# Layer norm's rows: two VectorE instructions, or GpSimd's offset and ScalarE, chosen by the planner

## The chip, the cores and the metric

The kernel runs on one core of a Trainium2 chip. The metric is the device time of one execution in microseconds (us), the median over runs.

## The reference

One decoder layer in fp32 with pre-norm residuals: 32 sequences of 256 tokens, width 256. Cut to what matters:

```python
def _layernorm(x, axis=-1, eps=1e-05):
    m = jnp.mean(x, axis=axis, keepdims=True)
    v = jnp.var(x, axis=axis, keepdims=True)
    return (x - m) / jnp.sqrt(v + eps)

x = x + _L0_attn_ref(_layernorm(x), Wq, Wk, Wv, Ws, Wg, Wo, qconv_w, kconv_w, vconv_w, gnorm_w)
x = x + _L0_xattn_ref(_layernorm(x), ctx_1024, ctx_1024, mask, W_q, W_k, W_v, W_proj, b_proj)
x = x + _L0_ffn_ref(_layernorm(x), gate_w, Wu, Wv, Wo)
```

The first step is a gated causal linear attention with short convolutions of q, k and v (4 heads), the second a cross attention of 16 heads over 77 context rows, the third a mixture of 8 experts of which each token takes the best 2. Each begins with a layer norm without weights, so there are 3 x 32 = 96 norms of 256 rows by 256 columns.

## The kernel before

The tokens of one sequence lie as two tiles of 128 partitions by 256 columns (NTT = 2). Three kinds of stage run over the sequences: `self_attention` (5 sequences in flight), `cross_attention` (3 in flight) and `experts` (two sequences at a time, the last two alone). Each stage is written as a Python generator. Before every piece of work it yields what it wants to use, as an engine and a cost in ns, or a list of such wishes between which it may be put.

A planner (`Flow`) runs these generators against a small model of the engines: at each step it starts the wish that could begin first. Where a thread offers a list, it takes the wish that would end first by the model, in which `LATER` adds 700 ns to VectorE's and 500 ns to ScalarE's end. `BOTH` means VectorE and `PAIR` GpSimd, each holding a port that the two share. `best_order` lays the whole kernel out 70 times with shifted ranks of the stages, keeps the order that ends first by the model, and `decoder_layer` then writes the instructions out in that order. So the order on every engine follows from the planner's costs, and a changed cost or choice anywhere can move instructions everywhere.

The layer norm is `layernorm_T`. Per tile, VectorE makes the statistics (`ln_st`, `ln_mv`, lines 690 and 691). `rsqrt` lets GpSimd add eps and take the power -0.5 (`rs_r`, lines 670 and 671). GpSimd then makes the offset `ln_off` = -mean x rstd (line 696, two small instructions), and ScalarE makes the row `ln_h` = x x rstd + offset (line 702, one pass per tile). `turn_to` transposes `ln_h` on TensorE into `hT_ps` (line 680), and `copy` moves that to SBUF as `hT_a`, `hT_x` or `hT_e`, on ScalarE (line 638) or VectorE (line 640), as the planner finds. The projections, the queries or the experts' products read it from there.

Other names that matter here: `y` (the convolution's taps, line 824 on VectorE, or `tap` on ScalarE with a sum on GpSimd), `RzT` (running sums at line 912 and their reciprocals at line 918), `E` (a clamp, line 900, on VectorE or GpSimd), `cap` (a mask, line 1119), `cv_qk` and `cv_v` (line 840), the softmax `s` of the cross attention (ScalarE, line 1211; its product with `s_rs` at line 647 on VectorE or GpSimd), and the routing of the experts (`wt_ps`, line 1362). Line 647 holds all the products which `combine` places on VectorE or GpSimd.

Of the kernel before, what the change touches and what calls it, by code (L numbers as in the profile page):

```python
# [12 lines left out]
F32 = mybir.dt.float32  # L13
U8 = mybir.dt.uint8
AF = mybir.ActivationFunctionType
ALU = mybir.AluOpType
# [3 lines left out]
P = 128  # L20
# [23 lines left out]
PE, DVE, ACT, POOL, SP = "PE", "DVE", "ACT", "POOL", "SP"  # L44

BOTH, PAIR = "BOTH", "PAIR"
# [28 lines left out]
def act(columns, pointer=False):  # L75
    return 75 + 0.82 * columns + (80 if pointer else 0)
# [286 lines left out]
def decoder_layer(  # L363
# [27 lines left out]
    nc = tc.nc  # L391
    B, T, D = x.shape
    S2 = ctxT.shape[2]
    ND = D // P
    NTT = T // P
# [4 lines left out]
    small = ctx.enter_context(tc.tile_pool(name="small", bufs=6))  # L400
# [23 lines left out]
    def lay_out(flow, nc, const, work, small, dram, psum):  # L424


        def take(tag, uses=1, name=None):
            shape = shapes[tag]

            kind = tag if isinstance(shape, tuple) else "f"  # L430
            buf = yield Take(kind, uses)
            dtype = F32
            if kind == tag:
                dtype = shape[2] if len(shape) > 2 else F32
                shape = shape[1]
            buf.tile = work.tile(
                shape, dtype, tag=f"{kind}{buf.slot}", name=name or tag, bufs=1
            )
            return buf
# [194 lines left out]
        def copy(to, source, columns, scale=None):  # L634

            engine, _ = yield [(ACT, act(columns)), (DVE, dve(columns))]
            if engine == ACT:
                nc.scalar.activation(to, source, AF.Copy, scale=1.0 if scale is None else scale)  # L638
            elif scale is None:
                nc.vector.tensor_copy(to, source)  # L640
            else:
                nc.vector.tensor_scalar(to, source, scale, None, ALU.mult)
# [23 lines left out]
        def rsqrt(var, n):  # L666

            r = small.tile([P, n], F32, tag=f"rs_r{n}", name="rs_r")
            yield POOL, 700 + 155 * n
            nc.gpsimd.tensor_scalar(r, var, EPS, None, ALU.add)  # L670
            nc.gpsimd.tensor_tensor(r, r, mhalf[:, :n], ALU.pow)  # L671
            return r

        def turn_to(src, tag, done):

            ps = yield from fill("brief", turns(4), tag)
            pv = halves(ps.tile)
            for c in range(ND):
                for t in range(2):
                    nc.tensor.transpose(pv[:, c, ts(t, P)], src[:, t, ts(c, P)], ident)  # L680
            done.drop()
            return ps, pv

        def layernorm_T(xt, hT):

            st = small.tile([P, NTT, 6], F32, tag="ln_st", name="ln_st")
            mv = small.tile([P, NTT, 2], F32, tag="ln_mv", name="ln_mv")
            for t in range(NTT):
                yield DVE, 550
                nc.vector.bn_stats(st[:, t, :], xt[:, t, :])  # L690
                nc.vector.bn_aggr(mv[:, t, :], st[:, t, :])  # L691
            rstd = yield from rsqrt(mv[:, :, 1], NTT)
            off = small.tile([P, NTT], F32, tag="ln_off", name="ln_off")
            yield POOL, 460
            for t in range(NTT):
                nc.gpsimd.tensor_scalar(  # L696
                    off[:, t : t + 1], mv[:, t, :1], rstd[:, t : t + 1], -1.0, ALU.mult, ALU.mult
                )
            h = yield from take("h", name="ln_h")
            for t in range(NTT):  # L700
                yield ACT, act(D) + 205
                nc.scalar.activation(  # L702
                    h.tile[:, t, :], xt[:, t, :], AF.Identity, bias=off[:, t : t + 1],
                    scale=rstd[:, t : t + 1],
                )
            ps, pv = yield from turn_to(h.tile, "hT_ps", h)
            yield from copy(hT, pv, 512)
            ps.drop()
# [79 lines left out]
        def self_attention(n):  # L788
# [3 lines left out]
            xt = xs[n].tile  # L792
            hT = yield from take("hT_a", 4)
            yield from layernorm_T(xt, hT.tile)
            ready = [flow.event() for _ in range(2)]
            prods = [None, None]
# [308 lines left out]
        def cross_attention(n):  # L1105
# [47 lines left out]
            xt = xs[n].tile  # L1153
            hT = yield from take("hT_x")
            yield from layernorm_T(xt, hT.tile)
            ps = None
            for c in range(ND):
# [122 lines left out]
        def experts(n, count):  # L1280
# [6 lines left out]
            for b in range(count):  # L1287
                yield crossed[n + b]
                yield from layernorm_T(xs[n + b].tile, hT.tile[:, :, b * T : (b + 1) * T])
# [297 lines left out]
```

## Time and profile before

| what | value |
|---|---|
| median of 3 runs | 1367.16 us (1366.28 to 1367.6) |
| the profiled execution's own time | 1367.22 us |
| span of its profile | 1365.4 us |
| granted TensorE clock, mean | 0.989 |
| TensorE busy | 1316.1 us (96%) |
| VectorE busy | 1145.0 us (84%) |
| ScalarE busy | 1040.9 us (76%) |
| GpSimd busy | 634.2 us (46%) |
| `ln_h` on ScalarE (line 702) | 192 instructions, 110.8 us, 597 ns each |
| `ln_off` on GpSimd (line 696) | 192 instructions, 61.1 us, 335 ns each |
| `rs_r` power on GpSimd (line 671) | 128 instructions, 128.1 us, 1001 ns each |

A busy share is an average over the span: the first microseconds, in which only attentions run, and the last, in which only experts are left, have other limits than the middle. Matrix instructions overlap and their ends are modelled, so a TensorE that is busy all the time is not one at its peak. DVE is VectorE, ACT ScalarE, POOL GpSimd, PE TensorE and PEld its weight loads. In the waits, `A <- B` says that A's engine sat idle until B was done.

### The profile page before, as it was taken

To read this page: it belongs to the slowest core of one execution; us is meant where nothing else is said; L and a number is where in the kernel's file an instruction comes from. 1 tells how busy PE (TensorE), PEld (TensorE's weight loads), DVE (VectorE), ACT (ScalarE), POOL (GpSimd) and SP (SyncE) were. 2 spreads that over 40 slices of the span, in tenths; PEclk is the share of its full clock that TensorE was granted. 3 is DMA by queue.
4 is the path that set the end of the run, shared out by engine and by line. 5 is a ranking of instruction groups with operands and counts; after the bars stand their busy time and mean duration, and the time that the engine had idled before them with its cause. 6 is when DMAs were issued, how large, how long until landed. Compare 5 with 4: busy or idle time off the path is not lost.

```text
span 1365.4 us, 27161 instructions
## 1 busy us (share of the span) xinstructions
PE 1316.1 (96%) x9345; PEld 971.0 (71%) x9345; DVE 1145.0 (84%) x2268; ACT 1040.9 (76%) x4160; POOL 634.2 (46%) x805
## 2 busy tenths in 40 slices
PE   6989989999999999999999999999999999999898
PEld 5767766676868776876778678678676876757665
DVE  6999999777887976998789889998988799966554
ACT  4668898867878876886888678788888786886741
POOL 1546654524465724347543555554444355534220
PEclk9899999999999999999999999999999999999999
DMA  4600010122111122111121120111111211021110
GB/s 129 139 2 2 13 19 4 30 63 64 42 40 44 27 58 55 49 29 32 48 51 39 34 48 3 42 35 19 33 43 48 64 29 34 17 60 45 43 40 24
DMA packets 134202, 55.91 MB, mean 41 GB/s; under 512 B 106168, under 2 KB 125880, under 8 KB 134064
## 3 DMA queue, kind: packets, MB, share of 16 engines
q1 hardware_dynamic: 134064, 54.17, 16.7%
q8 instruction: 74, 1.21, 0.4%
q14 instruction: 64, 0.52, 0.1%
HBM read 42.37 MB, written 11.79 MB: 40 GB/s over the span
## 4 chain that ended last, share of the span: by engine, by line
PE 67%; DVE 25%; ACT 5%; POOL 2%; issue 1%; DMA 0%; ACTq 0%; DVEq 0%; POOLq 0%
PE ev_ps L716 8%; PE u_ps L716 8%; PE eo_ps L1461 6%; DVE y L824 5%; PE cp_ps L739 4%; PE eT_ps L1241 3%; PE av_ps L1260 3%; DVE RzT L918 3%; PE pj_ps L725 3%; PE pr_ps L716 3%; PE wo_ps L725 3%; PE sc_ps L1183 3%; PE ov_ps L782 3%; PE Q_ps L716 3%; PE hT_ps L680 2%; PE s_ps L725 2%
## 5 line engine op out<-in xcount | busy, mean ns | idle before, releaser
L1211 ACT ACTIVATE s<-s,s_mx 128x77 f32<-128x77 f32 x1024 | 359.0, 356 | 38.3 <-DVE s_mx L1206 38.0
L1211 ACT ACTIVATION_READ_ACCUMULATOR s<-s,s_mx 128x1 f32 x1024 | 201.5, 197 | 0.0
L824 DVE SCALAR_TENSOR_TENSOR y<-pr_ps,conv,y 128x254 f32<-128x254 f32 (+2 forms) x368 | 149.1, 469 | 4.7 <-ACT y L811 4.5
L671 POOL TENSOR_TENSOR rs_r<-rs_r,mhalf 128x2 f32<-128x2 f32 (+1 forms) x128 | 128.1, 1001 | 10.7
L702 ACT ACTIVATE ln_h<-xs,ln_off,rs_r 128x256 f32<-128x256 f32 x192 | 110.8, 597 | 22.8 <-POOL ln_off L696 21.3
L1191 DVE TENSOR_TENSOR s<-sc_ps,cap 128x616 f32<-128x616 f32 x128 | 98.7, 784 | 26.9 <-PE sc_ps L1183 26.7
L716 PE MATMUL ev_ps<-hT_e,ev_s 128*128 128x512 f32 (+1 forms) x272 | 120.8, 572 | 0.1
L716 PE MATMUL u_ps<-hT_e,eu_s 128*128 128x512 f32 (+1 forms) x272 | 119.1, 571 | 0.4 <-DVE y L824 0.4
L647 POOL TENSOR_TENSOR esT<-e_th,wB 128x512 f32<-128x512 f32 x55 | 73.3, 1335 | 93.0 <-DVE e_th L1415 74.1
L1461 PE MATMUL eo_ps<-eo_s,esT 128*128 128x256 f32 x480 | 115.6, 384 | 0.0
L670 POOL TENSOR_SCALAR rs_r<-ln_mv 128x2 f32<-128x2 f32 x96 | 25.6, 267 | 185.6 <-DVE ln_mv L691 167.2
L918 DVE RECIPROCAL RzT<-RzT 128x256 f32<-128x256 f32 x64 | 110.7, 1733 | 0.0
L1461 PEld LDWEIGHTS eo_ps<-eo_s,esT 128*128 128x128 f32 x480 | 87.4, 190 | 14.0 <-issue 3.3
L968 ACT ACTIVATE ok<-ok,ok_mx 128x64 f32<-128x64 f32 x256 | 87.4, 344 | 8.9 <-DVE ok_mx L965 8.9
L1241 PE MATMUL eT_ps<-cst,s 128*128 128x128 f32 x640 | 88.3, 278 | 3.8 <-POOL s L647 1.7
L1206 DVE TENSOR_REDUCE s_mx<-s 128x16 f32<-128x1232 f32 x64 | 91.1, 1423 | 0.8
L1241 PEld LDWEIGHTS eT_ps<-cst,s 128*128 128x128 f32 x640 | 75.6, 143 | 18.4 <-issue 7.0
L647 POOL TENSOR_TENSOR s<-s,s_rs 128x1232 f32<-128x1232 f32 x28 | 63.2, 2257 | 53.7 <-DVE s_rs L1217 53.6
L690 DVE BATCH_NORM_STATS2 ln_st<-xs 128x6 f32<-128x256 f32 x192 | 78.4, 408 | 8.0 <-DMA xs<-in_x_dram 7.6
L716 PEld LDWEIGHTS u_ps<-hT_e,eu_s 128*128 128x128 f32 x272 | 49.3, 190 | 42.3 <-issue 39.0
L758 DVE TENSOR_TENSOR cp<-cp_ps,cst 128x768 f32<-128x768 f32 x78 | 72.5, 939 | 6.1 <-PE cp_ps L739 6.1
L638 ACT ACTIVATE eT<-eT_ps 128x1024 f32<-128x1024 f32 x64 | 65.6, 1026 | 14.6 <-PE eT_ps L1241 14.4
(167 smaller groups left out, 3432.5 us busy)
## 6 DMA issues: line engine op xcount, KB each, us to landing
wB<-wd SPq DMA_DIRECT2D x60, 256.0 KB
Vb<-spread_v SPq DMA_DIRECT2D x32, 320.0 KB
xs<-in_x_dram SPq DMA_DIRECT2D x32, 256.0 KB
out_dram<-xs SPq DMA_DIRECT2D x32, 256.0 KB
cx<-in_ctx_dram SPq DMA_DIRECT2D x32, 77.0 KB
spread_v<-V SPq DMA_DIRECT2D x32, 77.0 KB
spread_v<-zeros SPq DMA_DIRECT2D x2, 309.0 KB
mk<-in_mask_Bx1xSxS_bk_dram SPq DMA_DIRECT2D x32, 19.2 KB
```

The costliest lines, as they stand in the source:

```text
L647: engines[engine].tensor_tensor(to, a, b, op)
L671: nc.gpsimd.tensor_tensor(r, r, mhalf[:, :n], ALU.pow)
L702: nc.scalar.activation(h.tile[:, t, :], xt[:, t, :], AF.Identity, bias=off[:, t : t + 1], scale=rstd[:, t : t + 1],)
L716: nc.tensor.matmul(ps, lhsT=w[:, d], rhs=hT[:, d, :], start=(d == 0), stop=(d == ND - 1))
L725: nc.tensor.matmul(pv[:, t, :], lhsT=hT[:, d, ts(t, P)], rhs=w[:, d, :], start=(d == 0), stop=(d == n - 1),)
L824: nc.vector.scalar_tensor_tensor(y.tile[:, u, s:], now, by, y.tile[:, u, s:], ALU.mult, ALU.add)
L918: nc.vector.reciprocal(Rz.tile[:, c, :], Rz.tile[:, c, :])
L1191: nc.vector.tensor_tensor(sv[:, 2 * a : 2 * a + 2], got[a].tile[:, :, : ND * QR * S2].rearrange("p r (h k) -> p r h k", k=S2), cap.tile[:, ...
L1206: nc.vector.tensor_reduce(mx.rearrange("p (q h) -> p q h", h=QH), sv, AX.X, ALU.max, negate=True)
L1211: nc.scalar.activation(sv[:, h // QH, h % QH, :], sv[:, h // QH, h % QH, :], AF.Exp, bias=mx[:, h : h + 1], accum_out=sm[:, h : h + 1],)
L1241: nc.tensor.transpose(flat[:, ts(NTT * i + t, P)], s[t].tile[:, column : column + P], ident)
L1461: nc.tensor.matmul(halves(ps.tile)[:, t, :], lhsT=sT.tile[:, d, ts(NTT * b + t, P)], rhs=eo_s[:, d, :], start=(d == 0), stop=(d == NEC - 1),)
```

## The change

`layernorm_T` takes the tile for `ln_h` ahead of the offset and then offers the planner two ways. In the first, VectorE makes each tile's row in one instruction, (x - mean) x rstd, with mean and rstd as one value per partition; no offset is needed, and the pair is booked at 620 ns with the shared port. In the second, everything is as it was: GpSimd's offsets (460 ns) and ScalarE's passes. Line numbers behind it grow by 8.

```diff
             rstd = yield from rsqrt(mv[:, :, 1], NTT)
-            off = small.tile([P, NTT], F32, tag="ln_off", name="ln_off")
-            yield POOL, 460
-            for t in range(NTT):
-                nc.gpsimd.tensor_scalar(
-                    off[:, t : t + 1], mv[:, t, :1], rstd[:, t : t + 1], -1.0, ALU.mult, ALU.mult
-                )
             h = yield from take("h", name="ln_h")
-            for t in range(NTT):
-                yield ACT, act(D) + 205
-                nc.scalar.activation(
-                    h.tile[:, t, :], xt[:, t, :], AF.Identity, bias=off[:, t : t + 1],
-                    scale=rstd[:, t : t + 1],
-                )
+            engine, _ = yield [(BOTH, 620), (POOL, 460, ACT, 2 * act(D) + 410)]
+            if engine == BOTH:
+                for t in range(NTT):
+                    nc.vector.tensor_scalar(
+                        h.tile[:, t, :], xt[:, t, :], mv[:, t, :1], rstd[:, t : t + 1],
+                        ALU.subtract, ALU.mult,
+                    )
+            else:
+                off = small.tile([P, NTT], F32, tag="ln_off", name="ln_off")
+                for t in range(NTT):
+                    nc.gpsimd.tensor_scalar(
+                        off[:, t : t + 1], mv[:, t, :1], rstd[:, t : t + 1], -1.0,
+                        ALU.mult, ALU.mult,
+                    )
+                for t in range(NTT):
+                    yield ACT, act(D) + 205
+                    nc.scalar.activation(
+                        h.tile[:, t, :], xt[:, t, :], AF.Identity, bias=off[:, t : t + 1],
+                        scale=rstd[:, t : t + 1],
+                    )
             ps, pv = yield from turn_to(h.tile, "hT_ps", h)
```

## The prediction

> **What bounds the kernel.** I read the page's busy shares and slices first, then the chain that ended last, then busy time by stage, then TensorE's waits by stage, and last a timeline around one layer norm.
>
> ```profile
> PE 1316.1 (96%) x9345; PEld 971.0 (71%) x9345; DVE 1145.0 (84%) x2268; ACT 1040.9 (76%) x4160; POOL 634.2 (46%) x805
> PE   6989989999999999999999999999999999999898
> DVE  6999999777887976998789889998988799966554
> PE 67%; DVE 25%; ACT 5%; POOL 2%; issue 1%; DMA 0%; ACTq 0%; DVEq 0%; POOLq 0%
> ```
>
> TensorE is busy for all but 49.3 us of 1365.4, and the change touches none of its instructions. So 49.3 us is the most that there is to win, and less in truth: nothing can start before the first input lands, and the last output leaves after TensorE's last product. VectorE is second on the chain (25%); ScalarE, which gives work away, has 5%. Where TensorE stands idle is told by the stages (the columns are length, then busy time and count of each engine):
>
> ```profile
> core 0: us, PE busy (x) PEld busy (x) DVE busy (x) ACT busy (x) POOL busy (x), PEclk, DMA share, GB/s
> 0.00:250.00 250.00, 218.05 (x1621) 170.85 (x1623) 228.43 (x448) 188.52 (x730) 130.41 (x162) 0.96 0.18 43
> 250.00:1200.00 950.00, 943.12 (x6800) 695.43 (x6798) 822.69 (x1614) 757.23 (x3051) 463.66 (x588) 1.00 0.17 40
> 1200.00:1365.40 165.40, 154.91 (x928) 104.71 (x926) 93.91 (x208) 95.11 (x382) 40.09 (x56) 0.97 0.17 42
> ```
>
> The idle time is 32.0 us in the first 250, only 6.9 in the next 950, and 10.5 at the end. In the first stage VectorE is busy for 228 of 250 us, more than TensorE's 218: VectorE sets the pace there, since no expert products exist yet to fill TensorE. In the middle TensorE is full. What ended its waits on the layer norm, stage by stage (total, times, longest), with the other large one of the head:
>
> ```profile
> PE hT_ps L680 <- ACT ln_h L702: 9.2, 4, 6.8
> PE v_ps L880 <- DVE cv_v L840: 7.6, 3, 6.7
> ...
> PE hT_ps L680 <- ACT ln_h L702: 2.0, 3, 1.1
> ...
> PE hT_ps L680 <- ACT ln_h L702: 0.9, 2, 0.5
> ```
>
> The norm costs TensorE 12.1 us in all, of which 6.8 is the wait for the very first one.
>
> **What is removed, added and moved.** The planner (`best_order`, 70 tries) runs anew, so the order of everything shifts. The built program's order says how: 60 of 96 norms go to VectorE and 36 keep the old form. TensorE has the same 5609 matrix instructions, and its changes between tilings of the array are 451 where 454 were. I take its work as unchanged.
>
> *ScalarE.* 120 instructions of the row L702 go, at 597 ns: -71.6 us; other moves (12 fewer taps, 8 fewer copies of hT and aoT, a few more of others) give -7, so about 962 us. *GpSimd.* 120 of L696 at 335 ns go, -40.2; it takes on 6 more s products (2257 ns), 5 clamps E (2025 ns), 5 ok products and others, +28: 622 us. Neither engine sets the end, so both savings are worth nothing as such.
>
> *VectorE.* 120 instructions tensor_scalar of 128x256 from SBUF to SBUF arrive. No such row exists before. The nearest are the same operation in other widths (min/median/max in ns), and a 256-column statistic of the same input (busy us, mean ns):
>
> ```profile
> L900 DVE TENSOR_SCALAR E<-E x9: 412/429/1400, 13.3 to 1066.1; 128x512 f32<-128x512 f32 x9
> L1119 DVE TENSOR_SCALAR cap<-mk x32: 174/232/1365, 30.6 to 1262.5; 128x154 f32<-128x154 uint8 x32
> ```
>
> ```profile
> L690 DVE BATCH_NORM_STATS2 ln_st<-xs 128x6 f32<-128x256 f32 x192 | 78.4, 408 | 8.0 <-DMA xs<-in_x_dram 7.6
> ```
>
> Between the medians 429 (512 columns) and 232 (154) the line gives 232 + 102 x 0.55 = 288 ns for 256 columns. About 0.09 of that lies under the next instruction's start, as the timeline shows of its neighbours. The means (634 and 317) stand above the medians by 205 ns x 9 and 85 ns x 32, that is 111 ns for each of the 41: some ran while a GpSimd instruction ran, and took up to 1.4 us. So one multiply holds VectorE for 0.20 to 0.41 us (the upper end is the 408 of a 256-column statistic, or a multiply that meets GpSimd more often); I take 0.288 - 0.09 + 0.111 = 0.31, near the clamp and cap rows, as the operation is theirs. That is 37 us on VectorE. It is paid back in part, by the counts in the order: 6 fewer s products (1607 ns), 5 ok products (748), 5 clamps (634) and some others, -29.0; 12 more taps (469 ns), 8 more copies (690) and others, +15.7; net -13.3. So VectorE goes from 1145 to about 1169 us (86%), 1156 to 1181 between the ends.
>
> The Trainium skill ("SBUF — State Buffer", "Who interferes with whom") says that a tensor_scalar which uses both ports and a GpSimd instruction lock each other out for the whole instruction, which speaks against this change. By that rule alone, my estimate would be 120 x 0.46 (GpSimd's share) x about 0.65 us (half of its common 1.3 us product) = 36 us of waiting in place of the 13 that the rows give, unless the planner, which books the pair as one port, keeps them apart.
>
> *The head.* I summed both orders up to what TensorE needs of VectorE, each instruction at the mean time that its row holds the engine. Before, VectorE's queue runs furthest ahead at the first routing transposes (wt_ps L1362): 230 us of VectorE against 190 of TensorE, 36.6 us counting the starts (3.4 and 6.8 us). That is more than the idle time seen, since TensorE's changes of tiling are left out; I use the difference alone. After, the largest lead is 35.2 us with a multiply at 0.20, 37 at 0.30, 38.2 at 0.35 and some 39.4 at 0.41. Only 9 of the first 17 norms are on VectorE, and the shed products balance them. So -1.4 to +2.8 us, and I take 0.
>
> *One norm's path.* It loses GpSimd's two offsets and ScalarE's two passes and gains two multiplies. The late norm at 1284 us:
>
> ```profile
> 1284.81 0.71 POOL L671 TENSOR_TENSOR rs_r<-rs_r,mhalf 128x2 f32<-128x2 f32 x1
> 1285.62 0.50 POOL L696 TENSOR_SCALAR ln_off<-ln_mv,rs_r 128x1 f32<-128x1 f32 x2
> 1285.92 0.60 ACT L702 ACTIVATE ln_h<-xs,ln_off,rs_r 128x256 f32<-128x256 f32 x1 [0.76 <-POOL ln_off L696]
> 1286.77 0.58 ACT L702 ACTIVATE ln_h<-xs,ln_off,rs_r 128x256 f32<-128x256 f32 x1
> 1287.41 0.55 PE L680 MATMUL hT_ps<-cst,ln_h 128*128 128x128 f32 x3 [0.51 <-ACT ln_h L702]
> ```
>
> The power ends at 1285.52 and the second pass at 1287.35, 1.83 us later, with a softmax row of ScalarE in between. Two multiplies end some 0.6 us after the power: 1.2 us less. In the first norm the power ends at 5.72 and the second pass at 7.21; two multiplies would end near 6.25: 0.96 less, and the wait of 6.8 us falls by as much. The activation table's load, which stood behind the first input, waits for nothing in the new order, so it stays hidden.
>
> *Sum.* Start -1.0. Head 0. Middle: the 2.0 us of waits on the norm, of which I credit half, -1.0; the rest of the middle is full and gives nothing. Tail: the last five norms are all on VectorE, which is idle for 71 of 165 us there; two waits on a norm are exposed, and the routing and expert steps behind them start earlier: 2 x 1.2 = -2.4. Together -4.4: a span of 1361.0. The profiled execution took 1367.22 for its span of 1365.4, 1.8 outside it, and agrees with the median of 1367.16. So 1362.8 us. A difference under 0.2% (2.7 us) is about what a measurement of this kernel cannot tell from none.
>
> **The rivals.** *VectorE's queue decides: slower.* The two multiplies stand in VectorE's queue, where six conv taps in a row take 2.33 us and a pair of reciprocals (L918, 1733 ns each) 3.4; the transposes of hT, then the projections, wait behind them. ScalarE had shorter neighbours (356 ns). For it: VectorE's 25% of the chain, and stages of 95% (800 to 900, 1100 to 1200). Against it: 950 us in which TensorE lost 6.9, so that a late norm has other products ahead of it. Some 45 of the 60 lie in the middle; if 6 to 8 of them each hold TensorE for 1 to 2 us, that is +6 to +16, and a multiply at 0.41 adds 2.8 in the head. It decides once more than 3 norms are exposed that way: 1375 us, up to 1382.
>
> *Nothing shows.* The head is bound by the same VectorE sum, the middle by TensorE, and the few us at the ends are lost in the new order: 1365 to 1369.
>
> *The whole wait goes.* If the relieved ScalarE and GpSimd also deliver the head's inputs (E, cv_v's tanh, qk) sooner, half of the head's 25 us beyond the start could go: 1367 - 4 - 12 = 1351. Against it is VectorE's unchanged sum there.
>
> *The change does not do what it says.* The planner might have left all norms on ScalarE; the order with 60 on VectorE rules this out.
>
> **How the numbers follow.** Small gain, 1362.8 (its own range 1359 to 1364.4): 0.35. Large gain near 1351: 0.08. Nothing: 0.20. VectorE's queue: 0.37. Faster by over 0.2% is 0.43, within 0.20, slower 0.37. The range reaches from 1350 to 1380, with about 1 in 10 left out on either side: the large gain's lower part and the queue's upper part.
>
> **What would show it.** Right: hT_ps waiting on ln_h for under 8 us in all, first product near 6.1 us, TensorE's busy time within 5 us of 1316, idle in the first 250 us within 3 of 32, and the new row near 290 ns at the median and 400 in the mean. Wrong: a mean above 500 ns (port waits); hT_ps waiting on VectorE rows for over 10 us, or idle in the middle above 15 us (the queue); idle in the head below 25 (the large gain).

## The result: 2.6 us slower, and the profile after

| kernel | median | lowest to highest | runs |
|---|---|---|---|
| before | 1366.99 us | 1366.28 to 1367.76 | 12 |
| after | 1369.63 us | 1368.43 to 1370.88 | 12 |

The ratio is 1.0018, with an interval of 1.0010 to 1.0025. A gain of 4.4 us was forecast. The kernel became 2.6 us slower. That lies at the edge of what was called "no difference", but the interval leaves no gain.

The page of the kernel after, with its busy times and the chain that ended last:

```profile
PE 1318.6 (96%) x9345; PEld 972.5 (71%) x9345; DVE 1180.6 (86%) x2383; ACT 978.5 (72%) x4024; POOL 617.8 (45%) x700
PE 63%; DVE 27%; ACT 5%; POOL 2%; issue 1%; DMA 1%; SPq 0%; DVEq 0%; POOLq 0%; ACTq 0%
```

VectorE has 1180.6 us where 1169 was forecast, and two more per cent of the chain. TensorE's busy time rose by 2.5 us with the same number of instructions. Busy time by stage of the kernel after (columns as before: length, then PE, PEld, DVE, ACT and POOL):

```profile
0.00:250.00 250.00, 215.97 (x1558) 170.74 (x1558) 227.82 (x445) 172.25 (x681) 119.63 (x140) 0.95 0.18 43
250.00:1200.00 950.00, 940.83 (x6762) 691.64 (x6762) 838.02 (x1690) 707.82 (x2915) 457.70 (x509) 1.00 0.17 41
1200.00:1367.80 167.80, 161.77 (x1029) 110.12 (x1027) 114.78 (x250) 98.45 (x431) 40.47 (x52) 0.99 0.15 38
```

Length less TensorE's busy time is its idle time. With the before values it gives where the 2.4 us of span came from:

| part | before | after | change | forecast |
|---|---|---|---|---|
| TensorE idle, 0 to 250 | 31.95 | 34.03 | +2.1 | -1.0 |
| of that, until the first product | 6.77 | 6.33 | -0.44 | -1.0 |
| TensorE idle, 250 to 1200 | 6.88 | 9.17 | +2.3 | -1.0 |
| TensorE idle, from 1200 | 10.49 | 6.03 | -4.5 | -2.4 |
| TensorE busy | 1316.1 | 1318.6 | +2.5 | 0 |
| span | 1365.4 | 1367.8 | +2.4 | -4.4 |

Taken together the idle time is the same, 49.3 and 49.2 us: what the end won, the head and the middle lost. The 2.4 us by which the span grew are about what TensorE's busy time grew by. The three stretches are cut by time, so they do not hold quite the same work in both kernels: from 1200 us on there are 928 matrix instructions before and 1029 after.

What ended TensorE's waits in the first 250 us of the kernel after (total, times, longest):

```profile
PE hT_ps L680 <- DVE ln_h L697: 6.9, 2, 6.3
PE cp_ps L747 <- DVE gate L939: 4.7, 1, 4.7
PE ET_ps L680 <- POOL E L908: 3.6, 1, 3.6
PE ov_ps L790 <- DVE cp L776: 3.1, 1, 3.1
...
PE hT_ps L680 <- ACT ln_h L710: 0.9, 1, 0.9
```

The same view of 250 to 1200 us:

```profile
PE ev_ps L724 <- DVE e_th L1414: 1.5, 2, 0.9
...
PE hT_ps L680 <- DVE ln_h L697: 0.6, 2, 0.3
...
PE hT_ps L680 <- ACT ln_h L710: 0.5, 1, 0.5
```

From 1200 us on no wait on a norm is left. So the waits on the norm did fall, from 12.1 us to 6.9 + 0.9 + 0.6 + 0.5 = 8.9. The head's other idle time has new names: the waits on `gate`, the clamp `E` and `cp` stand where the wait of 7.6 us on `cv_v` stood before. The path of the norm became shorter, and the order around it is another one.

The new row in the kernel after: its instructions (min/median/max in ns), and its group (busy us, mean ns):

```profile
L697 DVE TENSOR_SCALAR ln_h<-xs,ln_mv,rs_r x120: 317/407/1434, 5.9 to 1338.4; 128x256 f32<-128x256 f32 x120
```

```profile
L697 DVE TENSOR_SCALAR ln_h<-xs,ln_mv,rs_r 128x256 f32<-128x256 f32 x120 | 55.1, 500 | 6.4 <-POOL rs_r L671 6.1
```

The median is 407 ns where 288 was taken, and the excess of the mean over the median is 500 - 407 = 93 ns where 111 was taken. VectorE also stood idle for 6.1 us until a power was done.

### The profile page after: what moved, and what is told of

Its sections match the earlier page's. It is cut to its first block, busy times and chain, and to the rows that moved or that the text cites. A ratio compares the mean times of both kernels' runs of the same rounds, so it can differ in the third digit from the quotient of the medians.

```text
span 1367.8 us, 27006 instructions
## 1 busy us (share of the span) xinstructions
PE 1318.6 (96%) x9345; PEld 972.5 (71%) x9345; DVE 1180.6 (86%) x2383; ACT 978.5 (72%) x4024; POOL 617.8 (45%) x700
## 4 chain that ended last, share of the span: by engine, by line
PE 63%; DVE 27%; ACT 5%; POOL 2%; issue 1%; DMA 1%; SPq 0%; DVEq 0%; POOLq 0%; ACTq 0%
PE ev_ps L724 7%; PE u_ps L724 6%; PE eo_ps L1469 6%; DVE y L832 5%; PE eT_ps L1249 4%; PE cp_ps L747 4%; PE av_ps L1268 4%; PE pr_ps L724 3%; PE Q_ps L724 3%; PE pj_ps L733 3%; PE wo_ps L733 3%; DVE RzT L926 3%; PE s_ps L733 2%; PE ov_ps L790 2%; DVE s L1199 2%; PE sc_ps L1191 2%
## 5 line engine op out<-in xcount | busy, mean ns | idle before, releaser
L1219 ACT ACTIVATION_READ_ACCUMULATOR s<-s,s_mx 128x1 f32 x1024 | 197.8, 193 | 0.0
L832 DVE SCALAR_TENSOR_TENSOR y<-pr_ps,conv,y 128x255 f32<-128x255 f32 (+2 forms) x380 | 153.3, 469 | 8.3 <-ACT y L819 8.0
L671 POOL TENSOR_TENSOR rs_r<-rs_r,mhalf 128x2 f32<-128x2 f32 (+1 forms) x128 | 125.3, 979 | 10.7
L647 POOL TENSOR_TENSOR s<-s,s_rs 128x1232 f32<-128x1232 f32 x34 | 77.4, 2276 | 41.6 <-DVE s_rs L1225 41.6
L908 POOL TENSOR_SCALAR E<-E 128x512 f32<-128x512 f32 x28 | 58.5, 2092 | 64.0 <-ACT E L905 63.2
L724 PEld LDWEIGHTS ev_ps<-hT_e,ev_s 128*128 128x128 f32 x272 | 48.2, 190 | 39.9 <-issue 35.2
## 6 DMA issues: line engine op xcount, KB each, us to landing
mk<-in_mask_Bx1xSxS_bk_dram SPq DMA_DIRECT2D x32, 19.2 KB
```

The lines of the kernel that those rows point to most:

```text
L647: engines[engine].tensor_tensor(to, a, b, op)
L724: nc.tensor.matmul(ps, lhsT=w[:, d], rhs=hT[:, d, :], start=(d == 0), stop=(d == ND - 1))
L832: nc.vector.scalar_tensor_tensor(y.tile[:, u, s:], now, by, y.tile[:, u, s:], ALU.mult, ALU.add)
L1219: nc.scalar.activation(sv[:, h // QH, h % QH, :], sv[:, h // QH, h % QH, :], AF.Exp, bias=mx[:, h : h + 1], accum_out=sm[:, h : h + 1],)
```

## The experiments

Three theories were set against each other. A: VectorE's queue, made longer by a multiply that costs more than was thought, takes the time. B: the order that the planner's search drew decides, and the norm has little part in it. C: the order drawn after the change works only because norms left ScalarE. Each verdict below is against runs of the kernel before on the same chip, whose medians were 1366.34 to 1366.94 us.

### The orders, crossed

`e1_after_order_scalar` keeps the plan and the order of the kernel after, and emits the 60 norms of VectorE in the old form at the same places:

```diff
             if engine == BOTH:
+                off = small.tile([P, NTT], F32, tag="ln_off", name="ln_off")
                 for t in range(NTT):
-                    nc.vector.tensor_scalar(
-                        h.tile[:, t, :], xt[:, t, :], mv[:, t, :1], rstd[:, t : t + 1],
-                        ALU.subtract, ALU.mult,
-                    )
+                    nc.gpsimd.tensor_scalar(...)
+                for t in range(NTT):
+                    nc.scalar.activation(...)
```

> The order of the changed kernel, but the 60 norms that went to VectorE are made by GpSimd's offset and ScalarE at the same places of the order. Theory A (VectorE's longer queue costs the time: the multiply holds it for 0.43 us instead of the 0.31 that I took, 120 times, and 13 of them wait for GpSimd): back to 1367 us or below. Theory B (the newly planned order costs it, whatever engine makes the rows): stays at 1369 to 1370. Theory C (the order only works because the norms left ScalarE): 1371 to 1378, since 60 norms' passes stand in ScalarE's queue at places that were not booked for them.

`e2_before_order_vector` keeps the order and the bookings of the kernel before, and emits the same 60 norms (24 of the self attention, 16 of the cross attention, 20 of the experts) as multiplies:

```diff
+VECTOR = {'a': (0, 1, 3, ...), 'x': (0, 5, 7, ...), 'e': (0, 1, 3, ...)}
...
+            vector = key[1] in VECTOR[key[0]]
...
                 yield ACT, act(D) + 205
-                nc.scalar.activation(...)
+                if vector:
+                    nc.vector.tensor_scalar(...)
+                else:
+                    nc.scalar.activation(...)
```

> The order of the kernel before, but the same 60 norms by their stage and sequence (24 of attention, 16 of cross attention, 20 of experts) are made by VectorE's two instructions, without the offset. Theory A: 51 us more on VectorE and nothing else moved: slower than 1367 by 3 us or more, with the idle time of TensorE growing in the first 250 us by 4 to 6. Theory B: the engine does not matter: 1366 to 1368. If a shorter path of the norm is worth something by itself: 1364 to 1366.

Measured: 1412.23 us for the first, ratio 1.0336 (1.0322 to 1.0350), and 1393.55 us for the second, 1.0199 (1.0185 to 1.0213). Both crossings lose far more than the change itself moved. The first lies beyond all three theories, of which C with 1371 to 1378 came nearest. The second is slower as A had it, but not where A put it: TensorE's idle time in the first 250 us is 32.4 us against 31.95, and in the middle it is 19.8 against 6.9. What ended TensorE's waits in the first, over its whole span:

```profile
PE hT_ps L680 <- ACT ln_h L703: 16.7, 25, 7.0
PE cp_ps L753 <- DVE gate L945: 4.0, 1, 4.0
PE ET_ps L680 <- POOL E L914: 3.6, 1, 3.6
...
PE ov_ps L796 <- DVE cp L782: 3.1, 1, 3.1
```

And in the second:

```profile
PE hT_ps L681 <- DVE ln_h L706: 19.8, 17, 6.3
```

In the first, ScalarE in its turn waited 27.9 us for GpSimd's offsets. The order after the change leaves the old form little slack, and the order before it leaves VectorE little. C holds as far as it goes: in the order after the change, giving the norm to VectorE is worth 42.6 us. Of the 42.1 us between the two spans, 17.9 are busy time of TensorE, which stays unexplained.

The first run shows one thing more. The head's waits on `gate`, `E` and `cp` stand there at 4.0, 3.6 and 3.1 us, where the kernel after has 4.7, 3.6 and 3.1, though no norm's row is made on VectorE in this run. They belong to the order, not to VectorE's new work.

The second run lost 27 us to what the rival "VectorE's queue decides" spoke of, late rows of VectorE, where the order was not made for them. Part of it is waiting for GpSimd, since that plan did not book the shared port: 18 of its 120 multiplies took over 0.7 us, where 12 did in the kernel after. The run does not part the two. In the order that the planner made with the choice in hand such waits are nearly absent, as the views above show.

### Which order is it?

The search was then run with other seeds, and without any shift of ranks:

```diff
-    rng = random.Random(0)
+    rng = random.Random(1)
```

> The kernel before with another seed of the planner's search (1 for 0): the same choices on offer, another order. Theory B: differs from 1367 by 2 us or more either way, as the order alone moves the time by as much as the change did. Theory A: within 1.5 us of 1367.

> The changed kernel with seed 1. Theory A: 2 to 4 us above the kernel before with seed 1. Theory B: no fixed distance to it, anywhere from 6 below to 6 above.

```diff
-ORDERS, MOVED, BY = 70, 20, 0.3
+ORDERS, MOVED, BY = 1, 20, 0.3
```

> The kernel before with one order instead of 70, the one that moves no rank. The changed kernel's order is just that one: none of the 69 moved ones was better by the planner's model, with seed 0 and with seed 1 alike. Theory B, now narrower (the search found something for the kernel before and nothing for the changed one): 1369 to 1373, so that against it the changed kernel is no loss. Theory A (VectorE's longer queue): 1366 to 1368, as the search is worth nothing.

Measured: `before_seed1` 1367.48 us, ratio 1.0011 (1.0002 to 1.0020), and `after_seed1` 1369.34, 1.0021 (1.0012 to 1.0030). The first is within 1.5 us of 1367, as A had it; B had it 2 us off or more. The second turned out to be the kernel after once more: with seeds 0 and 1 the search finds nothing that its model likes better than the first order, with no rank shifted. It serves as a repeat: its profile had TensorE busy for 1319.7 us, against 1318.6.

`before_unmoved`, the kernel before at just that first order, took 1413.56 us, 1.0350 (1.0336 to 1.0364), far above what either theory had. Its first two stages:

```profile
0.00:250.00 250.00, 201.11 (x1413) 158.47 (x1413) 207.26 (x388) 170.47 (x636) 117.58 (x147) 0.90 0.17 42
250.00:1200.00 950.00, 926.08 (x6595) 678.73 (x6590) 801.13 (x1574) 727.24 (x2953) 459.54 (x574) 0.99 0.17 40
```

TensorE is idle for 48.9 us in the head and 23.9 in the middle. So at unshifted ranks the change is worth 1413.6 - 1369.6 = 44 us, close to the 42.6 of the crossing. But the kernel before did not run at unshifted ranks. Its search had already won 46.6 us by shifting them, with the norms on ScalarE as they were.

### The price of the multiply

`after_immediates` keeps everything, the order on each engine too, and gives the multiply the constants 0 and 1 in place of mean and rstd. It leaves the normalisation of those 60 norms out, and with it the wait for the power:

```diff
-                        h.tile[:, t, :], xt[:, t, :], mv[:, t, :1], rstd[:, t : t + 1],
-                        ALU.subtract, ALU.mult,
+                        h.tile[:, t, :], xt[:, t, :], 0.0, 1.0, ALU.subtract, ALU.mult,
```

> The changed kernel's order with the multiplies' mean and rstd replaced by the constants 0 and 1: it leaves out the normalisation of the 60 norms on VectorE and their wait for rs_r. It tells what a multiply costs without values per partition: 290 ns at the median if those make the difference from the clamp's row, 407 if it is the width or the layout. Theory A: at 290 ns it takes 14 us off VectorE, and the time falls to 1367 or below, more so as the wait for the power is gone too. Theory B: 1368 to 1370.

`after_one_pointer` gives the pair's first multiply the constant 0 and rstd, and the second the mean and the constant 1:

> The changed kernel's order; of each pair of multiplies the first takes a constant for the mean and the second a constant for rstd, so each has one value per partition instead of two; it leaves out half of the norm for the 60 norms on VectorE. With constants alone the row took 285 ns at the median, with two values per partition 407. If each value costs the same: 345. If one is enough to lose the faster form: 405. If only the pair does: 285.

Measured: 1366.04 us for the first, 0.9997 (0.9988 to 1.0006), and one execution of 1369.44 for the second. The row in the first:

```profile
L697 DVE TENSOR_SCALAR ln_h<-xs x120: 230/285/1377, 4.6 to 1336.0; 128x256 f32<-128x256 f32 x120
```

And the two rows in the second:

```profile
L696 DVE TENSOR_SCALAR ln_h<-xs,rs_r x60: 254/346/1436, 5.8 to 1337.9; 128x256 f32<-128x256 f32 x60
...
L699 DVE TENSOR_SCALAR ln_h<-xs,ln_mv x60: 334/346/1434, 6.1 to 1338.2; 128x256 f32<-128x256 f32 x60
```

With none, one and two values per partition the same instruction takes 285, 346 and 407 ns at the median: 61 ns for each, the first of the three cases on record. The forecast's 288 was the price without them. Taking the values and the wait away returns 1369.63 - 1366.04 = 3.6 us. The profile shows 1.44 of it at the start (first product at 4.89 us in place of 6.33). There 1.29 is the wait for the power (the first multiply starts at 4.57 us in place of 5.86), and no step of the prediction could have had that. So the time is what theory A had set, but at most 2.3 us of it are left for a VectorE that is busy for 19.2 us less; between the two profiles, with spans of 1367.8 and 1365.5 us, only 1.0. Its waits in the head are nearly those of the kernel after:

```profile
PE hT_ps L680 <- DVE ln_h L697: 5.4, 2, 4.9
PE cp_ps L746 <- DVE gate L938: 4.1, 1, 4.1
PE ET_ps L680 <- POOL E L907: 3.6, 1, 3.6
...
PE ov_ps L789 <- DVE cp L775: 3.1, 1, 3.1
```

Idle time in its first 250 us is 250 - 217.57 = 32.4, that is 1.6 less than in the kernel after, and the start explains 1.44. So the head's new idle time came with the order, not with the multiply's price, as the first crossing also showed.

`after_twice` goes the other way and issues each multiply twice:

```diff
-                for t in range(NTT):
+                for t in (0, 0, 1, 1):
```

> The changed kernel's order with each of the 120 multiplies on VectorE issued twice: 51 to 55 us more on VectorE. Its price per us on VectorE, by which the mis-sized multiply is judged: theory A (VectorE's queue sets the pace in the first 250 us and is close to it later): 1380 to 1395, a third to a half of what is added. Theory B (only the order matters): 1370 to 1375.

Measured: 1405.19 us, 1.0279 (1.0264 to 1.0295). VectorE gained 1232.9 - 1180.6 = 52.3 us and the kernel lost 35.6: 0.68 us per us, where 19.2 us less had brought at most 2.3. Both theories had it lower. Waits of TensorE on the norm in the middle of this run:

```profile
PE hT_ps L680 <- DVE ln_h L697: 11.1, 20, 1.5
```

Twenty waits there, where the kernel after has two. By these two runs the planned order has room for VectorE up to about the work that it has, and little beyond: the price is nearly flat on one side and steep on the other. The second multiply also lengthens each norm's own path, and the run does not part that from the load on VectorE. The rest of the 35.6 us lies in work behind the norms that is late too; TensorE was also busy for 13.1 us more, which I can't explain.

### The truer price, and more tries

`after_cost860` tells the planner what a pair holds when a port wait is added:

```diff
-            engine, _ = yield [(BOTH, 620), (POOL, 460, ACT, 2 * act(D) + 410)]
+            engine, _ = yield [(BOTH, 860), (POOL, 460, ACT, 2 * act(D) + 410)]
```

> The changed kernel with the pair booked at 860 ns, two times the 0.43 us for which a multiply held VectorE, instead of 620; 47 norms stay on VectorE, and the search settles on a moved order. Theory A (a pair costs more than the planner was told): 1365 to 1368. Theory B: 1366 to 1368 as well, for its moved order; if it is above 1369, neither is the whole cause.

Measured: 1375.77 us, 1.0079 (1.0065 to 1.0094), with 47 norms on VectorE. Both theories had it at 1368 at most, and above 1369 neither was to be the whole cause. A truer price made the time worse: it put 13 norms back on ScalarE and drew another order, and the run does not part the two.

Then 400 tries in place of 70, seed 2, for both kernels:

> The changed kernel with 400 orders and seed 2; it settles on a moved order, with 56 norms on VectorE. Theory B: 1364 to 1368, the loss goes when the search finds something. Theory A: 1369 or more, as VectorE has nearly the same to do.

> The kernel before with 400 orders and seed 2, the same search that brought the changed kernel to 1364.7 us. Theory B: it falls as well, to 1362 to 1366, so that with equal search the change gives nothing that can be told, or a small loss. If the change is a gain of its own at equal search: 1366 or more.

Measured: after 1364.67 us, 0.9985 (0.9976 to 0.9993), which is faster than both kernels; before 1367.45, 1.0006 (0.9998 to 1.0015). B was right for the first and wrong for the second, which did not fall. What was on record as the sign of a gain of the change's own, 1366 or more, did come; but this is one draw of each kernel, and the next section shows how little that says. The first stage of the faster one, which has 56 norms on VectorE:

```profile
0.00:250.00 250.00, 219.37 (x1551) 171.10 (x1552) 227.88 (x442) 176.00 (x692) 116.59 (x134) 0.95 0.18 43
```

The head has 30.6 us of idle time where the kernel after has 34.0, with the multiply at the same 408 ns, and its waits on the norm are longer in all (12.8 + 0.9 us against 8.9). So the order made the difference, not the waits on the norm.

### How far draws spread

Other seeds at 70 tries each, the rest untouched:

> The kernel before with seed 2: a third order out of a search of 70. Theory B (each search draws its order, and the draw moves the time by several us): anywhere from 1360 to 1380, and not within 1 us of 1367 again. Theory A (VectorE's longer multiply costs the 2.6 us, orders out of a full search agree): within 1.5 us of 1367.

> The kernel before with seed 3. Theory B: 1365 to 1390, with 1367 near the lower end of what its searches of 70 bring. Theory A: within 1.5 us of 1367.

> The kernel before with seed 4. Theory B: 1365 to 1390, and over all seeds the kernel before is not faster than the changed kernel with the same seeds. Theory A: within 1.5 us of 1367.

> The changed kernel with seed 4, whose search of 70 does leave the order that moves no rank. Theory B: anywhere from 1362 to 1378. Theory A: 1368 to 1371, as for seeds 0 and 1.

> The changed kernel with seed 5, another moved order out of a search of 70. Theory B: 1362 to 1380, apart from seeds 0, 1 and 4 by several us. Theory A: 1368 to 1371.

| seed | before | after |
|---|---|---|
| 0 | 1367.0 | 1369.6 |
| 1 | 1367.5 (1.0002 to 1.0020) | 1369.3 (same program) |
| 2 | 1384.0 (1.0107 to 1.0138) | not run |
| 3 | 1365.0 (0.9978 to 0.9997) | not run: seed 0's program but for two neighbouring GpSimd instructions, which change places |
| 4 | 1375.8 (1.0051 to 1.0081) | 1373.8 (1.0043 to 1.0068) |
| 5 | not run | 1388.0 (1.0143 to 1.0177) |

Theory A missed in all five. B was right on the spread, though 1384.0 and 1388.0 lie above its ranges, and wrong that the kernel before would not be the faster one over all seeds. With nothing but the seed changed, each of the two kernels spreads over 19 us. In the seeds that both have (0, 1, 3 and 4, with 1369.6 for seed 3 of the kernel after), the means are 1368.8 and 1370.6; three of the four values after stand for one order, so they are two draws. A difference of 1.8 us between such draws does not tell whether the change as such gains or loses. The slowest, `after_seed5`, shows the waits that the rival spoke of, over its whole span:

```profile
PE hT_ps L680 <- DVE ln_h L697: 19.0, 10, 6.3
```

Seed 3 of the kernel before, without the change, is within 0.4 us of the fastest version found.

## Why the prediction was wrong, point by point

*What bounds the kernel.* Right. TensorE's 96% stayed, and all that moved lies in its idle time and in 2.5 us of its own.

*The multiply.* Mis-sized. A clean pair takes 0.73 us in the timeline, 0.365 each with the overlap, and with the excess of 0.093 one multiply holds VectorE for 0.46 us: 55 us for all, against the 37 of the sum and above the upper end of 0.41. The line through the clamp and the mask gave 288, and both of these rows use constants. The row to take was one with two values per partition, and the trace before had none. It had a hint: one instruction (line 601) with one such value took 470 ns at 512 columns, where the clamp's median was 429. The upper end came from the statistic's 408, with no excess added. The port term was right: 93 ns against 111, some 11 us of waiting in all, where the estimate from the Trainium skill's lock rule was 36. This error is worth at most 2.3 us of the 6.8 us between forecast and result. ScalarE's saving was mis-sized too (978.5 us against 962), without effect, as the sum gave it no worth.

*The start.* Misread. The sum compared the end of ScalarE's second pass with that of the second multiply. But TensorE's first product waits for the first row alone. Before:

```profile
6.12 1.09 ACT L702 ACTIVATE ln_h<-xs,ln_off,rs_r 128x256 f32<-128x256 f32 x2 [1.36 <-POOL ln_off L696]
6.77 1.39 PE L680 MATMUL hT_ps<-cst,ln_h 128*128 128x128 f32 x4 [6.77 <-ACT ln_h L702]
```

And after:

```profile
5.86 0.73 DVE L697 TENSOR_SCALAR ln_h<-xs,ln_mv,rs_r 128x256 f32<-128x256 f32 x2 [1.16 <-POOL rs_r L671]
6.33 1.22 PE L680 MATMUL hT_ps<-cst,ln_h 128*128 128x128 f32 x4 [6.33 <-DVE ln_h L697]
```

The two passes end at 7.21 us, but the product starts at 6.77. So the first wait fell by 0.44 us in place of 0.96. In the profile after, the first statistic also started 0.12 us later, and the dearer multiply took about as much.

*The head at 0, the middle at -1.0.* These failed, and not by the multiply or the norm's path. The waits on the norm fell by 3.2 us over the whole span, of the 4.4 that the sum credited; in the middle they fell from 2.0 to 1.1, as it had it. But the head became 2.1 us worse and the middle 2.3, by waits on `gate`, `E`, `cp` and `e_th` that are not the norm's. With a multiply at 285 ns the same order keeps nearly all of them, and with those norms on ScalarE it keeps the first three. The step that failed is the one that took the new order as good as the old: the sum credited only what the norm's own path would do, and let everything else stand, though each instruction had been put anew. Its one check was VectorE's lead in the head, which says how much VectorE has to do and not where the order leaves a hole. In its place the idle time of TensorE stayed at 49 us, where 4.4 less was forecast.

*The tail.* Right in sign, and too small: -4.5 against -2.4. No wait on a norm is left there, and those on the routing fell too. That is luck in part: the waits on a norm were only 0.9 us there, less than the 2.4 credited. And over the draws with a full search the idle time from 1200 us on is 5.4 to 13.7 us, with 6.0 and 10.5 among them, so the order moves it by more than this.

*TensorE's work at 0.* This is the other half of the miss. The sum took the work as unchanged, since the instructions are; TensorE's busy time rose by 2.5 us, about as much as the span. The same program showed 1318.6 and 1319.7 in two profiles, and the draws of the kernel before with a full search 1313.0 to 1320.4, so it goes with the order. Which neighbours cost it stays open.

*The rivals and the range.* "Nothing shows" came nearest: losses elsewhere in the new order ate what the ends gave. "VectorE's queue decides" did not: TensorE waited 6.9 + 0.6 us on VectorE's norms in all, 6.3 of it for the first, and idle time in the middle was 9.2 us where 15 would have shown it. The range of 1350 to 1380 held the time, but for reasons too narrow: no case in it was the draw itself, and two of the draws, one of each kernel, lie above it.

*What stays open.* Whether the change gains or loses with an equally good order: at 400 tries it is ahead, 1364.67 us against 1367.45, at 70 tries behind by 1.8 us in the mean, and both are within the spread.

## What to carry to other kernels

Where a planner or a search lays a kernel out, a small edit draws a new order, and one run before and after measures two draws: compare several seeds or a longer search on both sides before the edit gets the credit or the blame. An order fits the engines that it was made with, so swapping an operation's engine inside a finished order measures the order and not the operation. And price a VectorE instruction from a row with as many values per partition as it has, not only the same width.

## What the hardware showed

Each value per partition costs a tensor_scalar of 128x256 in fp32 another 61 ns on VectorE, whether it is the first or the second operand: 285, 346 and 407 ns.

Meeting GpSimd is not one thing. In the kernel after, 13 of the 120 multiplies began with or during a two-input product of 128x512 on GpSimd (line 647), and each of them ended 0.15 to 0.23 us after that product. They took 542 ns where little of it was left and 985 to 1434 ns otherwise. Three multiplies that began before such a product kept their time (364, 407 and 407 ns). One place:

```profile
1044.94 1.27 POOL L647 TENSOR_TENSOR xs<-xs,bp 128x512 f32<-128x512 f32 x1
1045.01 1.75 DVE L697 TENSOR_SCALAR ln_h<-xs,ln_mv,rs_r 128x256 f32<-128x256 f32 x2 [0.91 <-POOL rs_r L671]
```

The pair starts 0.07 us after the product and takes 1.75 us. Beside the small powers multiplies kept their time (380 to 418 ns), and mostly beside the clamp, which has one input:

```profile
638.35 2.07 POOL L908 TENSOR_SCALAR E<-E 128x512 f32<-128x512 f32 x1
...
639.23 0.73 DVE L697 TENSOR_SCALAR ln_h<-xs,ln_mv,rs_r 128x256 f32<-128x256 f32 x2
```

The pair runs wholly inside the clamp's 2.07 us and takes the 0.73 of a clean one. Five of the six multiplies inside a clamp took 317 to 409 ns in this trace; the sixth, begun 0.15 us after its clamp's start, took 606. In the second crossing four of five took 595 to 771 ns, and two of these ended 0.15 us after their clamp. So the clamp delays a multiply in some stretches of its course and not in others; why stays open. The rule of the Trainium skill weighed in the prediction ("SBUF — State Buffer", "Who interferes with whom"), that whoever issues first blocks the other for the whole instruction, fits the product's rows here and not all of the clamp's. There the measurement decides, with the caution that records of GpSimd are rough.
